# A gated graph network on Trainium2: all engines of the GRU stage in a written order, normalizing in halves, one staging place for two streams, weights turned in three places

## The chip, the core and the metric

The kernel runs on one core of a Trainium2 chip. The metric is device time in microseconds. The core's engines have names of their own in the profile: PE is TensorE (matmuls and transposes through the identity), ACT is ScalarE, DVE is VectorE, POOL is GpSimd, SP is SyncE, which here only issues DMAs.

## What is computed

The reference takes x [16, 1024, 128], an adjacency adj [16, 1024, 1024] of zeros and ones, a node mask (all ones) and weights. Two residual layers follow each other.

```python
# layer 0: pre-norm, four gated graph layers
h = relu(layernorm(x))
for i in range(4):
    m = adj^T @ (h @ weight[i])
    gx = m @ w_ih[i].T + b_ih[i];  gh = h @ w_hh[i].T + b_hh[i]
    r = sigmoid(xr + hr);  z = sigmoid(xz + hz);  n = tanh(xn + r * hn)
    h = (1 - z) * n + z * h
x = x + h * mask
# layer 1: pre-norm, four convolutions
h = relu(layernorm(x))
for i in range(4):
    h = batchnorm_over_batch_and_nodes(relu(adj @ (h @ W[i]) + b[i]))
out = x + h * mask
```

## The kernel before

There are two stages in one program. The GRU stage does layer 0, batch by batch, until about 1165 us; then the convolution stage does layer 1. The change lies in the GRU stage. A flag is computed beside it (`worst`, L1223): the largest low half of any word of adj, which says whether adj is exactly representable in the short type in which its rows are kept for layer 1. ACT reads such low halves with `glance` (L587), DVE with `look` (L611), one row block of 128 x 1024 at a time.

**Streams and clocks.** Two streams run against each other: A has the even batches, B the odd ones. One call of `half_step(one, two)` is a clock, counted from 3; at odd clocks `one` is A, at even clocks B. In a clock PE does the gates of `two` in two halves of 512 nodes (12 passes each, L982) and then the aggregation of `one` (32 matmuls of 128 x 512, L525): h, with nodes on the partitions, is split in a high and a low part, and each of the eight row blocks of adj meets both. h @ weight isn't computed: weight is folded into w_ih beforehand (`join_layer`, L487), so the gates take m through `w_mT`. A batch has four layers of one aggregation and one gate step each; a pair of batches takes eight clocks. I call the clock in which A does its fourth layer's gates 8k, for k = 1 to 7; there B aggregates its fourth layer. In 8k+1, B does its fourth gates and A aggregates the first layer of its next batch, and in 8k+2 B aggregates the first layer of its own.

**What a clock needs from the others.** ACT does for each half r = sigmoid (L994), tanh (L1000), z = sigmoid (L1001), and DVE the sums around them: two ahead of the tanh (L995, L996), then h − n (L1007, or L1005 in a batch's first layer), times z (L1008), plus n (L1009). Each gate has a single PSUM bank (`g_r`, `g_z`, `g_hn`, `g_xn`), so the second half's products wait until the first half's readers are done. The new h goes to node order through DRAM: DVE transposes blocks of 32 x 32 (L721), SP writes them out (L592) and reads them back (L599), ACT copies the high part (L915; L937 in a first layer, straight from y) and DVE subtracts to get the low part (L916, L941). At the end of an aggregation ACT copies m from PSUM in two halves (L954); the gates of the next clock need it.

**Work beside the gates.** A finished batch has its tail: sums with the mask (`tail_sums`), factors (a square root on ACT with its table load, L669), eight normalizing blocks (`norm_blocks`, ACT, L681), and stores. A coming batch has its x loaded, statistics, factors, and again eight blocks. An agenda, `at(clock, place, go)`, says in which clock and at which place of it each is issued; most are in the place "gap", between the halves of the aggregation. In 8k and 8k+1 the next batch's adjacency comes: `fetch` has SP load four row blocks of 512 KB into a staging tile of the stream (L573), POOL rounds them to the matmul's type (L578), ACT glances at them, and then the other four go into the same places. The low halves of A's last four are looked at by DVE, B's by ACT one clock later. The row blocks are also transposed on PE for layer 1, in the places where `feed.some` stands.

**What sets the order.** Up to clock 4 all engines run in the order written. From clock 5 on only PE, POOL and SP do (`tc.manual_schedule(engines=...)`, ahead of the loop); ACT and DVE are ordered by a scheduler, with `behind(...)` as a hint that something comes after a given instruction.

**Weights.** Three transposes give w_hhT (L470), three w_ihT (L474), one the graph weight (L479), each group with its own copy out; layer 1's are made halfway through clock 3's aggregation, layer 2's halfway through clock 4's, layer 3's after it.

Of the kernel before, what the change touches and what calls it, by code (L numbers as in the profile page):

```python
# [341 lines left out]
def exact_path(  # L342
# [123 lines left out]
    def turn_layer(prep, w_g, i):  # L466

        pt = tmp(f"pt_whh{i}")
        for g in range(3):
            nc.tensor.transpose(pt[:, g * P : (g + 1) * P], wns["hh", i][:, g, :], ident)  # L470
        nc.scalar.copy(w_hhT[:, i, :], pt[:, : 3 * P])
        pt = tmp(f"pt_wih{i}")
        for g in range(3):
            nc.tensor.transpose(pt[:, g * P : (g + 1) * P], wns["ih", i][:, g, :], ident)  # L474

        w_ihT = prep.tile([P, 3 * C], F32, tag="w_ihT", name=f"w_ihT{i}", bufs=1)
        nc.scalar.copy(w_ihT, pt[:, : 3 * P])
        pg = tmp(f"pt_g{i}")
        nc.tensor.transpose(pg[:, :P], w_g[:, i, :], ident)  # L479
        w_gT = prep.tile([P, P], F32, tag="w_gT", name=f"w_gT{i}", bufs=1)  # L480
        nc.scalar.copy(w_gT, pg[:, :P])
        turned[i] = w_gT, w_ihT
# [51 lines left out]
    with ExitStack() as st:  # L534
# [234 lines left out]
        written = [True]  # L769

        def behind(*inss):

            es = ExitStack()
            for ins in () if written[0] else inss:
                es.enter_context(tc.issue_after(ins.ins))
            return es

        class Stream:


            def __init__(self, first):
                self.b, self.i, self.tag = first, 0, "AB"[first % 2]
                self.opened, self.across, self.stage = None, False, None
                self.outs, self.split = [], []
# [31 lines left out]
            def load_ahead(self):  # L816
                self.next_x = load_x(self.b + 2, nc.gpsimd)

# [9 lines left out]
            def next_blocks(self):  # L828
                self.next_y = work.tile([P, N], F32, tag=f"y{self.tag}", name=f"y_in{self.b + 2}", bufs=1)
                norm_blocks(self.next_x, self.next_y, self.next_norm, range(NB))  # L830

            def plan(self, n, tail=None):

                if tail:
# [6 lines left out]
                    def blocks():  # L841
                        end["y"] = y_mid(b)
                        norm_blocks(xt, end["y"], end["norm"], range(NB))
# [4 lines left out]
                    at(n + 4, "gap", blocks)  # L848
                    at(n + 5, "mid", lambda: store_ymid(b, end["y"]))
                if self.b + 2 < B:  # L850
                    at(n + 5, "mid", self.next_load)
                    at(n + 5, "gap", self.next_sums)
                    at(n + 6, "gap", self.next_factors)
                    at(n + 7, "gap", self.next_blocks)

            def fetch(self):

                if self.i == 3 and self.b + 2 < B and not written[0]:
                    stage = turned_tile(f"stage{self.b + 2}").bitcast(F32)
                    self.stage = [stage[:, 2 * q : 2 * q + 2, :].rearrange("p a n -> p (a n)") for q in range(4)]  # L860
                    stage_rows(self.b + 2, self.stage, range(4))

            def first_four(self):
                if self.stage:
                    with behind(self.first_act):
                        glance(self.b + 2, self.stage, range(1))
                    self.rows = round_rows(self.b + 2, self.stage, range(4))

            def last_four(self):
                if self.stage:  # L870
                    with behind(self.first_act):
                        glance(self.b + 2, self.stage, range(1, 4))
                    stage_rows(self.b + 2, self.stage, range(4, NB))
                    self.rows += round_rows(self.b + 2, self.stage, range(4, NB))
                    b, stage, self.stage = self.b + 2, self.stage, None
                    if self is sb:

                        at(clock[0] + 1, "late", lambda: glance(b, stage, range(4, NB)))
                        return
                    with behind(self.last_dve):  # L880
                        for j in range(4, NB):
                            look(b, stage[j % 4], j)

            def take(self):
# [3 lines left out]
                return blocks_out(self.y, f"in{self.b}")  # L888

            def turned_away(self, i):  # L890

                return not written[0] and i < L

            def half_away(self, hf):

                if self.turned_away(self.i + 1 - hf):
# [11 lines left out]
            def split_back(self, g, *after):  # L908
                if self.outs:
                    cols = slice(g * HALF, (g + 1) * HALF)  # L910
                    hi, lo = (four_ways(t[:, cols]) for t in self.hw)
                    back = by_nodes(self.backs[g])
                    with behind(*after):
                        self.split = [
                            nc.scalar.copy(hi, back),  # L915
                            nc.vector.tensor_sub(lo, back, hi.bitcast(F32)),  # L916
                        ]
# [3 lines left out]
            def split_step(self):  # L921
                self.split = []
                if self.outs:
                    self.halves_back()
                    return
                nm = f"{self.b}_{self.i}"
                self.hw = hw_tiles(self.b, f"ghw{nm}")
                for g in range(NH):
                    if self.i > 0:
                        features_times(None, self.hT, self.hw, g, f"g{nm}")  # L930
                        continue
                    self.split_high(g)
                    self.split_low(g)
# [31 lines left out]
            def gate_step(self, hf, between=None, after=()):  # L965
# [26 lines left out]
                r = work.tile([P, HALF], F32, tag="r", name=f"r{nm}")  # L992
                z = work.tile([P, HALF], F32, tag="z", name=f"z{nm}")
                self.first_act = nc.scalar.activation(r, pr, AF.Sigmoid, bias=brz[:, 3 * i : 3 * i + 1])  # L994
                nc.vector.scalar_tensor_tensor(r, phn, b_hn(i), r, ALU.add, ALU.mult)  # L995
                self.mid_dve = nc.vector.tensor_add(r, pxn, r)  # L996
                if between:
                    between()
                with behind(*after[:1]):
                    nc.scalar.activation(r, r, AF.Tanh, bias=b_in(i))  # L1000
                self.last_act = nc.scalar.activation(z, pz, AF.Sigmoid, bias=brz[:, 3 * i + 1 : 3 * i + 2])  # L1001
                ho = self.new[:, cols]
                with behind(*after[1:]):
                    if across:
                        nc.vector.tensor_sub(four_ways(ho), hin, four_ways(r))  # L1005
                    else:
                        nc.vector.tensor_sub(ho, hin, r)  # L1007
                nc.vector.tensor_mul(ho, ho, z)  # L1008
                self.last_dve = nc.vector.tensor_add(ho, ho, r)  # L1009
# [4 lines left out]
            def finish(self):  # L1014
# [8 lines left out]
                ins = self.take()  # L1023
                h_in = self.hT
                outs = blocks_out(args[-1], f"out{args[0]}")
# [15 lines left out]

        def half_step(one, two, gated=None, halfway=None):

            feed.next_step()
            one.split = []
            if one.i == 0:
                two.fetch()
            due("ins")
            if one is sb and one.i == 0 or written[0] and one is sa:
                feed.jobs = transposes([(s.b, s.rows) for s in (sa, sb)])  # L1050
            if one.i > 0:
                one.split_step()
                two.fetch()
                feed.some(2)
            two.gate_step(0)
            two.half_away(0)
            two.first_four()
            if feed.full or (clock[0], "mid") in agenda:

                pace = small.tile([P, 1], F32, tag="pace", name=f"pace{clock[0]}")  # L1060
                nc.gpsimd.tensor_copy(pace, two.new[:, :1])
                feed.store()
                due("mid")
            due("outs")
            one.split_back(0, two.last_act, two.mid_dve)
            one.split_back(1, two.last_act, two.mid_dve)
            if one.i > 0:
                feed.some(1)
            two.gate_step(1, None, one.split)
            two.half_away(1)  # L1070
            with behind(two.first_act):
                due("late")
            if one.i == 0:
                feed.some(1)
            two.last_four()
            if gated:
                gated()
            if one.i == 0:
                with behind(two.last_m):
                    one.split_step()  # L1080
# [3 lines left out]
            with behind(two.last_act, two.last_dve, *one.split):  # L1084
                due("gap")
            feed.some(NB if written[0] and one is sa else 1)
# [6 lines left out]
        with tc.tile_pool(name="prep", bufs=1) as prep, tc.manual_schedule(engines=every):  # L1093
# [42 lines left out]
            turn_layer(prep, w_g, 0)  # L1136
# [58 lines left out]
            sb.agg_rows(range(4, NB))  # L1195

            def looks():
                for j in range(4, NB):
                    first_look(1, j, raw1[j])

            sa.plan(0)
            sb.plan(1)
            half_step(sa, sb, looks, lambda: turn_layer(prep, w_g, 1))
            join_layer(1)
            half_step(sb, sa, None, lambda: turn_layer(prep, w_g, 2))
            join_layer(2)
            turn_layer(prep, w_g, 3)
            join_layer(3)
        with tc.manual_schedule(engines={getattr(mybir.EngineType, e) for e in ("PE", "Pool", "SP")}):
            written[0] = False  # L1210
            for s in range(2, B // 2 * L):
# [302 lines left out]
```

## Time and profile before

| | us |
|---|---|
| median of three runs | 1789.59 (1788.88 to 1790.59) |
| the profiled execution | 1787.94 |
| its span | 1786.2 |
| PE busy in it | 1761.1 (99%) |
| DVE, ACT, POOL busy | 1254.0, 1107.5, 387.7 |
| time in which `g_r` waited for ACT's m | 30.6 in 61 waits of the weight load, the longest 1.8 |
| time in which ACT's glances waited for rows | 10.9 |

The granted TensorE clock is 0.998 in the profile. A line of the groups reads: source line, engine, operation, output <- inputs by the program's names, shapes, count, then busy time and mean duration in ns, then the idle time of the engine before them and what ended it. A line of the timeline reads: start and duration in us from the span's start, the engine, line and operation, the number of instructions in a row of that kind, and in brackets the idle time before with what ended it. Starts and durations of PE overlap, since its matmuls are pipelined; differences of starts are what counts there.

### The profile page before, as it was taken

The numbers are of one execution on the slowest core, as the hardware profiler recorded it, in microseconds if no ns is written. First come the engines' busy times: TensorE is split into PE (matmuls) and PEld (weight loads), VectorE is DVE, ScalarE is ACT, GpSimd is POOL, SyncE is SP. The second block draws the span as 40 slices with busy tenths as digits, with TensorE's granted clock in tenths as the row PEclk, the third lists the DMA queues.
The fourth block names the chain that finished last, engine by engine and source line by source line (L and its number), as shares of the span: only waits on it lengthen the run. The fifth ranks groups of instructions, "written<-read, shape, count | busy, mean of one in ns | idle before, by whom it ended". The sixth has DMA issues, their size and how long they took to land. (4 is left out here: it accounts for less than half of the span.)

```text
span 1786.2 us, 22134 instructions
## 1 busy us (share of the span) xinstructions
PE 1761.1 (99%) x6742; PEld 1193.5 (67%) x6742; DVE 1254.0 (70%) x2308; ACT 1107.5 (62%) x1717; POOL 387.7 (22%) x417
## 2 busy tenths in 40 slices
PE   9999999999999999999999999999999999999997
PEld 5556555565656565556565656577778888888886
DVE  7567867877776776877786776666666666666665
ACT  5346556556566555655655645476777767768765
POOL 4213323332322332422422333010100000000011
PEclk9999999999999999999999999999999999999999
DMA  7448677776776866776866867778766575767667
GB/s 254 113 123 294 168 205 245 205 210 224 224 200 216 229 198 203 244 204 185 286 173 172 266 185 215 274 266 313 276 220 246 206 248 208 248 224 239 244 216 270
DMA packets 362175, 399.09 MB, mean 223 GB/s; under 512 B 158028, under 2 KB 238704, under 8 KB 362048
## 3 DMA queue, kind: packets, MB, share of 16 engines
q1 hardware_dynamic: 341296, 322.54, 58.0%
q0 software_dynamic: 20224, 74.80, 11.4%
q8 instruction: 55, 0.90, 0.2%
q14 instruction: 72, 0.59, 0.1%
q10 hardware_dynamic: 528, 0.26, 0.0%
HBM read 266.95 MB, written 96.99 MB: 204 GB/s over the span
## 5 line engine op out<-in xcount | busy, mean ns | idle before, releaser
L525 PE MATMUL pm<-row,ghw 128*128 128x512 f32 x2048 | 506.8, 404 | 4.8 <-DVE ghw L916 4.1
L525 PEld LDWEIGHTS pm<-row,ghw 128*128 128x128 f32 x2048 | 384.6, 188 | 115.1 <-issue 29.4
L525 PE MATMUL pc_m<-wide,chw 128*128 128x512 f32 x1024 | 246.1, 395 | 0.0
L525 PEld LDWEIGHTS pc_m<-wide,chw 128*128 128x128 f32 x1024 | 190.4, 188 | 42.3 <-issue 4.3
L616 POOL CAST half<-row 128x1024 bf16<-128x1024 f32 x128 | 145.0, 1143 | 336.2 <-DMA adjT<-half 321.5
L525 PE MATMUL pc_g_r<-wide,chw 128*128 128x512 f32 x464 | 187.0, 403 | 0.3 <-ACT chw L502 0.3
L525 PE MATMUL pc_g_z<-wide,chw 128*128 128x512 f32 x464 | 181.0, 390 | 0.0
L995 DVE SCALAR_TENSOR_TENSOR r<-g_hn,vecs,r 128x512 f32<-128x512 f32 x128 | 95.1, 743 | 122.2 <-ACT r L994 76.5
L578 POOL CAST row<-stage 128x1024 fp32r<-128x1024 f32 x112 | 131.4, 1184 | 221.4 <-DMA stage<-in_adj_dram 171.3
L1001 ACT ACTIVATE z<-g_z,brz 128x512 f32<-128x512 f32 x128 | 87.4, 683 | 148.2 <-PE g_z L982 148.0
L954 ACT COPY m<-pm 128x512 f32<-128x512 f32 x128 | 68.5, 587 | 153.6 <-PE pm L525 153.5
L1000 ACT ACTIVATE r<-r,vecs 128x512 f32<-128x512 f32 x128 | 91.8, 717 | 114.4 <-DVE r L996 114.4
L1244 DVE CAST wide<-block 128x1024 fp32r<-128x1024 bf16 x160 | 109.8, 692 | 73.3 <-PE pc_m L525 49.4
L1244 DVE CAST wide<-packed 128x1024 fp32r<-128x1024 bf16 x160 | 110.2, 691 | 72.0 <-PE pc_g_z L525 54.0
L1007 DVE TENSOR_TENSOR h<-h,r 128x512 f32<-128x512 f32 x96 | 80.7, 841 | 100.2 <-ACT r L1000 100.2
L1242 ACT CAST wide<-packed 128x1024 fp32r<-128x1024 bf16 x96 | 100.6, 1048 | 58.9 <-PE pc_m L525 29.7
L982 PE MATMUL g_r<-m,w_mT 128*128 128x512 f32 x256 | 131.3, 594 | 3.5 <-ACT m L954 3.2
L1242 ACT CAST wide<-block 128x1024 fp32r<-128x1024 bf16 x96 | 100.6, 1049 | 52.6 <-PE pc_g_z L525 27.7
L982 PE MATMUL g_xn<-m,w_mT 128*128 128x512 f32 x256 | 130.8, 593 | 0.1
L982 PE MATMUL g_z<-m,w_mT 128*128 128x512 f32 x256 | 130.7, 592 | 0.0
L1292 DVE BATCH_NORM_STATS2 stats<-feat 128x6 f32<-128x512 f32 x128 | 84.1, 686 | 47.0 <-ACT feat L1291 45.9
L994 ACT ACTIVATE r<-g_r,brz 128x512 f32<-128x512 f32 x128 | 87.8, 686 | 37.4 <-PE g_r L982 37.1
(187 smaller groups left out, 2832.7 us busy)
## 6 DMA issues: line engine op xcount, KB each, us to landing
block<-adjT_d SPq DMA_DIRECT2D x256, 256.0 KB, 4.9
packed<-adjT_d SPq DMA_DIRECT2D x256, 256.0 KB, 5.6
stage<-in_adj_dram SPq DMA_DIRECT2D x120, 512.0 KB, 5.4
adjT_d<-adjT POOLq DMA_DIRECT2D x16, 2048.0 KB, 8.3
cross_h<-t_h SPq DMA_DIRECT2D x90, 256.0 KB, 3.2
n_h<-cross_h SPq DMA_DIRECT2D x360, 64.0 KB, 2.0
xmid_d<-x POOLq DMA_DIRECT2D x16, 512.0 KB, 6.0
y<-ymid_d POOLq DMA_DIRECT2D x16, 512.0 KB, 5.4
```

What stands on the lines that cost most here:

```text
L525: nc.tensor.matmul(pm[hf], hw[s][:, j * P : (j + 1) * P], rows[j][:, hf * HALF : (hf + 1) * HALF], start=(j == 0 and s == 0), stop=(j == N ...
L578: nc.gpsimd.tensor_copy(t, stage[j % 4])
L616: nc.gpsimd.tensor_copy(t, row.bitcast(F32))
L982: nc.tensor.matmul(po, wT[:, i, g * C : (g + 1) * C], rhs, start=start, stop=stop)
L994: self.first_act = nc.scalar.activation(r, pr, AF.Sigmoid, bias=brz[:, 3 * i : 3 * i + 1])
L995: nc.vector.scalar_tensor_tensor(r, phn, b_hn(i), r, ALU.add, ALU.mult)
L1000: nc.scalar.activation(r, r, AF.Tanh, bias=b_in(i))
L1001: self.last_act = nc.scalar.activation(z, pz, AF.Sigmoid, bias=brz[:, 3 * i + 1 : 3 * i + 2])
L1007: nc.vector.tensor_sub(ho, hin, r)
L1242: nc.scalar.copy(r, t)
L1244: nc.vector.tensor_copy(r, t)
L1292: nc.vector.bn_stats(stats[:, b * NH + hf, :], dst)
```

## The change

The order of the loop is written out for all engines up to clock 64; only the last gates are left to the scheduler as before. For that, `gate_step` is cut in pieces (`products`, `reset_gate`, `candidate`, `update_gate`, `less`, `mixed`), and the loop places them among the splits of the other stream (`high`, `low`), the glances, and the agenda's places.

- The eight normalizing blocks are issued four and four between r and tanh of both halves ("beside0", "beside1").
- The normalized x of the coming batch is transposed and written out (`ins_away`) at the end of clock n+7, not at the batch's change one clock later; the old batch's output goes out half by half in `half_away`.
- Both streams' rows are staged in one tile (`room[0]`). All four glances at the first rows follow z of the second half, and the second four rows are asked for after them. DVE's looks at A's last rows stand at the start of 8k+1; B's last glances in the gap of 8k+2.
- The places and counts of the row blocks' transposes on PE are others (`counts`); they begin at clock 8k+3.
- `turn_layer` becomes `turn_hh` and `turn_ih`; the latter puts w_ihT and the graph weight in one bank with one copy. hh is turned inside or halfway through an aggregation, ih ahead of one, the join comes halfway. Layer 3's turning moves to clock 5, and in clock 5 A's h takes the way through DRAM and not that over PE.
- `worst` follows the tail's sums instead of preceding a gate's chain, and in POOL's queue y's load for layer 1 comes before one store of transposed rows.

```diff
-    def turn_layer(prep, w_g, i):
+    def turn_hh(i):
         pt = tmp(f"pt_whh{i}")
...
+    def turn_ih(prep, w_g, i):
         pt = tmp(f"pt_wih{i}")
         for g in range(3):
             nc.tensor.transpose(pt[:, g * P : (g + 1) * P], wns["ih", i][:, g, :], ident)
-        w_ihT = prep.tile([P, 3 * C], F32, tag="w_ihT", name=f"w_ihT{i}", bufs=1)
-        nc.scalar.copy(w_ihT, pt[:, : 3 * P])
-        pg = tmp(f"pt_g{i}")
-        nc.tensor.transpose(pg[:, :P], w_g[:, i, :], ident)
-        w_gT = prep.tile([P, P], F32, tag="w_gT", name=f"w_gT{i}", bufs=1)
-        nc.scalar.copy(w_gT, pg[:, :P])
+        nc.tensor.transpose(pt[:, 3 * P :], w_g[:, i, :], ident)
+        both = prep.tile([P, 4 * C], F32, tag="w_both", name=f"w_both{i}", bufs=1)
+        nc.scalar.copy(both, pt)
...
-                    at(n + 4, "gap", blocks)
+                    at(n + 4, "beside0", lambda: blocks(0))
+                    at(n + 4, "beside1", lambda: blocks(1))
...
-                    at(n + 5, "gap", self.next_sums)
+                    at(n + 6, "start", self.next_sums)
                     at(n + 6, "gap", self.next_factors)
-                    at(n + 7, "gap", self.next_blocks)
+                    at(n + 7, "beside0", lambda: self.next_blocks(0))
+                    at(n + 7, "beside1", lambda: self.next_blocks(1))
+                    at(n + 7, "end", self.ins_away)
...
             def last_four(self):
                 if self.stage:
-                    with behind(self.first_act):
-                        glance(self.b + 2, self.stage, range(1, 4))
-                    stage_rows(self.b + 2, self.stage, range(4, NB))
-                    self.rows += round_rows(self.b + 2, self.stage, range(4, NB))
                     b, stage, self.stage = self.b + 2, self.stage, None
-                    if self is sb:
-                        at(clock[0] + 1, "late", lambda: glance(b, stage, range(4, NB)))
-                        return
-                    with behind(self.last_dve):
+                    glance(b, stage, range(4))
+                    stage_rows(b, stage, range(4, NB))
+                    self.rows += round_rows(b, stage, range(4, NB))
+
+                    def looks():
                         for j in range(4, NB):
                             look(b, stage[j % 4], j)
+
+                    if self is sa:
+                        at(clock[0] + 1, "start", looks)
+                    else:
+                        at(clock[0] + 1, "gap", lambda: glance(b, stage, range(4, NB)))
...
             def turned_away(self, i):
-                return not written[0] and i < L
+                return clock[0] > 3 and i < L
...
             due("ins")
+            due("start")
...
+            two.products(0)
+            two.reset_gate(0)
+            due("beside0")
+            two.candidate(0)
+            two.less(0)
+            one.high(0)
+            two.update_gate(0)
+            one.low(0)
+            two.mixed(0)
             two.half_away(0)
             two.first_four()
             if feed.full or (clock[0], "mid") in agenda:
+                mids(two)
+            one.high(1)
+            feed.some(counts[1])
+            two.products(1)
+            two.reset_gate(1)
+            due("beside1")
+            one.low(1)
+            two.candidate(1)
+            two.less(1)
+            two.update_gate(1)
+            two.last_four()
+            two.mixed(1)
+            two.half_away(1)
             due("outs")
+            due("gap")
+            due("end")
             if gated:
                 gated()
             one.agg_step(0)
             if halfway:
                 halfway()
-            feed.some(NB if written[0] and one is sa else 1)
+            feed.some(counts[2])
             one.agg_step(1)
             two.finish()
...
-            half_step(sa, sb, looks, lambda: turn_layer(prep, w_g, 1))
-            join_layer(1)
-            half_step(sb, sa, None, lambda: turn_layer(prep, w_g, 2))
-            join_layer(2)
-            turn_layer(prep, w_g, 3)
-            join_layer(3)
-        with tc.manual_schedule(engines={getattr(mybir.EngineType, e) for e in ("PE", "Pool", "SP")}):
+            first_step(sa, sb, looks, lambda: ahead(1))
+            first_step(sb, sa, lambda: turn_ih(prep, w_g, 2), lambda: ahead(2))
             written[0] = False
-            for s in range(2, B // 2 * L):
+            half_step(sa, sb, lambda: turn_ih(prep, w_g, 3), lambda: ahead(3))
+            half_step(sb, sa)
+            for s in range(3, B // 2 * L):
                 half_step(sa, sb)
                 half_step(sb, sa)
             assert not agenda, sorted(agenda)
+        with tc.manual_schedule(engines={getattr(mybir.EngineType, e) for e in ("PE", "Pool", "SP")}):
             sb.gate_step(0)
```

## The prediction

> **What bounds the kernel now.** I read in this order: busy shares, groups of TensorE (PE), waits, then PE's timeline around each wait. "Clock" means a half-step of the GRU loop, numbered as the code does (3 to 64); T0 is the first `g_r<-h` of a clock. The page and its groups:
>
> ```profile
> PE 1761.1 (99%) x6742; PEld 1193.5 (67%) x6742; DVE 1254.0 (70%) x2308; ACT 1107.5 (62%) x1717; POOL 387.7 (22%) x417
> L525 PE MATMUL pm<-row,ghw 128*128 128x512 f32 x2048 | 506.8, 404 | 4.8 <-DVE ghw L916 4.1
> ```
>
> PE is the engine, and its work is unchanged but for startup. So only its gaps count. A clock without a gap, and the next one:
>
> ```profile
> 279.04 1.02 PE L982 MATMUL g_r<-h,w_hhT 128*128 128x512 f32 x2
> ...
> 288.94 7.83 PE L525 MATMUL pm<-row,ghw 128*128 128x512 f32 x32
> 296.61 1.02 PE L982 MATMUL g_r<-h,w_hhT 128*128 128x512 f32 x2
> 298.61 1.12 PE L982 MATMUL g_r<-m,w_mT 128*128 128x512 f32 x2 [0.97 <-ACT m L954]
> ```
>
> From T0 to T0 it is 17.57 us (two halves of gates of 5.15, aggregation 7.27). Clock 17 waits for ScalarE's (ACT) copy of m; its T0s are 296.61 and 315.60, so it loses 1.42. Why the copy is late:
>
> ```profile
> 291.27 0.74 DVE L995 SCALAR_TENSOR_TENSOR r<-g_hn,vecs,r 128x512 f32<-128x512 f32 x1
> 293.24 0.72 ACT L1000 ACTIVATE r<-r,vecs 128x512 f32<-128x512 f32 x1 [1.97 <-DVE r L996]
> 293.87 1.04 ACT L587 ACTIVATE junk<-stage 128x1024 bf16<-128x1024 uint16 x1
> 294.91 3.17 ACT L681 ACTIVATE y_in<-x,ms_in,rs_in 128x128 f32<-128x128 f32 x8
> 297.99 1.04 ACT L954 COPY m<-pm 128x512 f32<-128x512 f32 x2
> ```
>
> ACT waited for VectorE (DVE), then did a glance and eight normalizing blocks, and m came after them. Every eighth clock has this queue. Another place is clock 59, where the flag's reduction stands on DVE ahead of the gates and waits for glances:
>
> ```profile
> 1040.23 0.30 DVE L1223 TENSOR_REDUCE worst<-low 128x1 f32<-128x144 f32 x1 [3.93 <-ACT junk L587]
> ...
> 1057.88 4.37 PE L525 MATMUL pm<-row,ghw 128*128 128x512 f32 x12 [2.08 <-DVE ghw L916]
> ```
>
> Over all: from clock 5's first aggregation matmul (94.91) to that of clock 64 (1146.99) lie 1052.08 us; 59 clocks of 17.573 are 1036.8. **15.3 us are stalls.** By clock: 59 has 4.3; 17 1.42, 33 1.23, 41 1.84, 57 1.43 (m or h_in late); 11, 19, 27, 35, 43, 49, 51 .4 to 1.0 (mostly the low half of hw, L916, late on DVE); 64 .6. Most clocks have none. The second stage (1165 on) is not touched.
>
> **What the Trainium skill says.** "Perfetto Trace Analysis", § Optimization Strategy, has one find the gaps on the most contended engine; the trace agrees that PE's 99% hides 15 us of them. "SBUF — State Buffer", § Who interferes with whom: a DVE instruction with two SBUF inputs and a GpSimd instruction that reads SBUF exclude each other. The trace agrees: L1008 takes .69 alone, 1.52 while GpSimd (POOL) casts rows at L578. "ScalarE: Activation LUTs", § What ACT_TABLE_LOAD costs, gives about 1283 ns; this trace has 1283. The number of loads stays.
>
> **Part 1, weights turned in three places.** Before, PE between its streams:
>
> ```profile
> 80.22 0.81 PE L487 MATMUL pt_wm<-w_ihT,w_gT 128*128 128x384 f32 x2
> 80.86 0.49 PE L470 MATMUL pt_whh<-ident,wn_hh 128*128 128x128 f32 x3
> 81.70 0.55 PE L474 MATMUL pt_wih<-ident,wn_ih 128*128 128x128 f32 x3 [0.35 <-ACT w_mT L488]
> 82.08 0.33 PE L479 MATMUL pt_g<-ident,w_g 128*128 128x128 f32 x1
> 83.04 0.91 PE L487 MATMUL pt_wm<-w_ihT,w_gT 128*128 128x384 f32 x2 [0.62 <-ACT w_gT L481]
> 83.79 1.39 PE L498 MATMUL hw_g<-ident,h 128*128 128x128 f32 x8
> 85.01 1.02 PE L982 MATMUL g_r<-h,w_hhT 128*128 128x512 f32 x2
> ```
>
> From clock 4's aggregation (real start 71.68) to clock 5's T0 at 85.01 are 13.33. After: aggregation 7.26, join .64, three hh transposes .33: 8.23. Layer 3's turning moves to clock 5, and its eight feature transposes go (1.2), since A's new hw then travels through DRAM; its halves are due only ten us later. So −5.1. Clock 3's aggregation (from 50.85) sheds seven transposes (.76) and two gaps of .4 from start to start (waits of .24), and gains three and four transposes (.33, .44): −.8. Clock 4 gains four ahead of its aggregation (+.44), clock 5 four and the join (.44 + .64 = +1.1). Layer 1's hh transposes at 37 add .33, mostly inside a wait of .47 at 44.8. Sum −.8 + .4 − 5.1 + 1.1 = **−4.4**, all on PE and so on the path. If the copies don't return in time for the transposes, one gap of .3 to .6 each comes back: bounds −5.0 to −3.0.
>
> **Part 2, written order, blocks in halves.** The eight blocks of 3.17 now lie four and four between r and tanh, where DVE's sums take longer anyhow; four cost ACT 1.6 and tanh waits for DVE until about then. ACT's queue in clock 8k (m copies, table load 1.28, r, four blocks, tanh, hi, z, hi, r, four blocks, tanh, z, four glances of 1.17) then, by the durations shown and T0=0: r0 ends 2.9, DVE's two sums 4.6, tanh0 to 5.3, second half's sums (DVE: less .69, lo, mul, add, transpose, two sums, one of them stretched by .8) to 11.0, tanh1, z1 to 12.3, glances to 17.0. m is wanted by 17.57+.24. No stall, slack .8. The late lows of clocks 8k+3 have written places ahead of the mul: stalls gone. L1223 moves to the tail's sums after the transpose: at most 1 us of DVE wait, PE unaffected. y's load in clock 60 moves past a store on POOL's queue: the .6 goes; if that were wrong, .6. All gains of this part: **−15.3**, if nothing new comes.
>
> **Part 3, one stage, glances after z.** This adds waits, which the trace of before doesn't show. The second four rows may only be fetched into a place when its glance is done; glances end at 13.5, 14.6, 15.8, 17.0, instead of beginning at 287.20 − 279.04 = 8.2. SP's queue holds nothing long ahead of them. SP's issues of rows and what it takes for one to land, from the line's own view:
>
> ```profile
> DMA to landing us min/median/max: 3.5/5.3/8.6
> ```
>
> Row 7, the last, took 4.0 to 5.8 before. So row 7 lands at 21.1 to 22.9, and its look (DVE, 1.2) ends at 22.3 to 24.0. In clock 8k+1 the looks stand on DVE ahead of the gates' first sum; behind them is the whole gate chain of stream B, so call their end s. From s: two sums 1.55 and tanh .7 (s+2.3), seven DVE instructions at pitches of .61 to .70 (4.6), tanh .65, z .6, four glances 4.7, .3 for hand-overs: ACT is free for m at s+13.1. T0 of 8k+2 is 35.14 and m may start at +.24 without loss. With s=22.4: 35.5−35.4=.1. **The unknown is contention**: B's rows land 24.5 to 29 and POOL casts them (L578) just while DVE does less, lo, mul, add of the first half; each that meets a cast is .8 longer (1.52 against .69). Two or three do: 1.6 to 2.4. Bounds: .1 (none meets, rows early) and 3.4 (s at 23.5, three met, and z0's bank, wanted by PE at 26.15, late by .6); not below zero: a gap can't be negative, and those of before are counted in part 2. I take 1.9 per eight clocks; seven pairs of batches (clocks 8 to 56): **+13.3**.
>
> What else moves costs nothing: next x dumped a clock earlier (two DVE transposes of .65 in a clock with several us of DVE idle; if that cover were gone, 1.3 per pair), t_out within clock 8k (same count); adjacency transposes start a clock later on PE (same number, in places that have their rows; a row missing would cost its landing, at most 1 us per pair).
>
> **Sum.** −4.4 −15.3 +13.3 = −6.4. The profiled execution took 1787.94 (span 1786.2): 1781.5. The median of the runs is 1789.59, 1.65 above it, so the forecast as a median is 1783.2.
>
> **Rivals.**
> Forecast (.45): new waits of about 1.9, range 1.0 to 2.5 per pair: 1777 to 1788.
> *Written order leaves nearly no stall* (.25): casts and sums miss each other, rows land early, .3 per pair: 2 instead of 13.3; −17.6: 1772. For it: rows' latencies at 3.5 are in the trace, and POOL is 22% busy. Against: before, L1008 averages .84, so a fifth of its instructions do meet a cast.
> *The one stage turns the chain late, slower* (.18): row 7 can't be asked for before the last glance, its look blocks DVE ahead of B's gates, B's glances wait for z, and m for these. At 3.9 per pair, 27.3 − 19.7 = +7.6: 1797. It decides from 19.7/7 = 2.8 per pair on (break-even), by .2% from 3.3. For it: every link is a written order with no slack beyond .2. Against: 3.9 needs the slowest landings and four meetings in each pair.
> *The waits just eat the gains* (.12): 2.8 per pair, 1789.6. That the change does nothing is thereby included.
> I count .2% (3.6 us) as what a measurement of this kernel can tell from no change. Below 1786.0 lie the second case and three quarters of the first: .59; between, the rest of the first and the last: .23; above 1793.2 the slower one: .18. Range 1771 to 1796: it leaves out the best of the second case and half of the slower one.
>
> **What would show it.** Right: clock 5's T0 about 5.5 earlier; no idle of PE at 8k+1 or 8k+3 and none after L1223; a wait of `g_r<-m` for ACT's m at T0 of clocks 10, 18, 26 and so on of 1 to 2.5. Wrong: that wait under .5 (second rival) or over 2.8 (third), DVE's first sum of 8k+1 beginning well before or after 22.4, L1223's reduction ahead of a gate again, or new gaps of PE in clocks without rows. The prediction is most wrong if the looks start late for a reason other than the row: then all seven pairs shift together.

## The result and the profile after

The changed kernel takes **1791.24 us** (median of 22 runs, 1788.37 to 1798.02) against 1788.39 for the kernel before (22 runs, 1785.18 to 1790.81): ratio **1.0020**, 95% interval 1.0014 to 1.0026. It is slower by 2.85 us; the forecast was 6.4 faster. The profiled execution took 1789.26 (span 1787.5), so the trace below shows 1.3 us of the difference. The changed kernel's runs spread more, and this execution lies 2.0 below their median. One run of the experiments, of the flag's reduction, fell in a slow state (3028.68 us at a granted clock of 0.556) and is left out of its median.

The page of the changed kernel, to be held against the first two lines shown of before (L525 is now L524, L916 L926):

```profile
PE 1759.3 (98%) x6734; PEld 1191.7 (67%) x6734; DVE 1305.9 (73%) x2310; ACT 1107.6 (62%) x1713; POOL 379.3 (21%) x417
L524 PE MATMUL pm<-row,ghw 128*128 128x512 f32 x2048 | 503.6, 402 | 0.7 <-DVE ghw L926 0.6
```

The late low halves (4.1 us of idle before) are down to 0.6. What PE waits for instead, from the waits of the whole span (total, times, longest):

```profile
PE g_z L993 <- ACT z L1020: 5.0, 8, 0.7
PE g_hn L993 <- DVE r L1012: 4.6, 6, 1.2
PE g_r L993 <- ACT m L955: 2.9, 4, 1.0
```

The first two are waits inside the gates; before, the first came to 0.8 and the second did not occur. PE's timeline of clock 17, the counterpart of the clock shown of before:

```profile
293.36 1.02 PE L993 MATMUL g_r<-h,w_hhT 128*128 128x512 f32 x2
...
301.54 1.13 PE L993 MATMUL g_hn<-h,w_hhT 128*128 128x512 f32 x2 [1.15 <-DVE r L1012]
...
304.18 1.12 PE L993 MATMUL g_z<-h,w_hhT 128*128 128x512 f32 x2 [0.66 <-ACT z L1020]
```

The m at the clock's start is in time now. But the second half's `g_hn` and `g_z` wait for the first half's banks. DVE's timeline of the same place two periods later (clock 33, T0 at 580.12) says why:

```profile
580.90 1.22 DVE L610 TENSOR_REDUCE low<-stage 128x1 f32<-128x1024 uint16 x1 [1.60 <-DMA stage<-in_adj_dram]
582.40 1.22 DVE L610 TENSOR_REDUCE low<-stage 128x1 f32<-128x1024 uint16 x1 [0.28 <-DMA stage<-in_adj_dram]
584.84 2.47 DVE L610 TENSOR_REDUCE low<-stage 128x1 f32<-128x1024 uint16 x2 [1.22 <-DMA stage<-in_adj_dram]
587.23 0.74 DVE L1012 SCALAR_TENSOR_TENSOR r<-g_hn,vecs,r 128x512 f32<-128x512 f32 x1
```

DVE, otherwise idle, waits for row after row of A, and the first sum of B's gates, which frees `g_hn`, stands behind the last of them.

A ledger of PE's lost time: for each clock the time from its T0 to the next, less the 17.573 of a clock without a gap, summed by the clock's place in its period (us; k = 1 to 7):

| | T0 of clock 6 | 8k+1 | 8k+2 | 8k+3 | 8k+4, 8k+5 | clocks 6 to 63 | T0 of clock 64 |
|---|---|---|---|---|---|---|---|
| before | 102.61 | 6.59 | 0.10 | 7.94 | 0 | 14.64 | 1136.48 |
| changed | 98.23 | 12.60 | 2.45 | 3.83 | 0.89 | 19.78 | 1137.25 |

The opening gives 4.37, the loop loses 5.14 more than before: +0.77 at clock 64. Here clock 3 is the first of the loop, and a loss is booked on the clock that holds it.

### The profile page after: what moved, and what is told of

It reads as the page before. It is cut to its first block, busy times and chain, and to the rows that moved or that the text cites. A ratio compares the mean times of both kernels' runs of the same rounds, so it can differ in the third digit from the quotient of the medians.

```text
span 1787.5 us, 22335 instructions
## 1 busy us (share of the span) xinstructions
PE 1759.3 (98%) x6734; PEld 1191.7 (67%) x6734; DVE 1305.9 (73%) x2310; ACT 1107.6 (62%) x1713; POOL 379.3 (21%) x417
## 5 line engine op out<-in xcount | busy, mean ns | idle before, releaser
L524 PE MATMUL pm<-row,ghw 128*128 128x512 f32 x2048 | 503.6, 402 | 0.7 <-DVE ghw L926 0.6
L524 PEld LDWEIGHTS pm<-row,ghw 128*128 128x128 f32 x2048 | 383.8, 188 | 106.6 <-issue 29.2
L524 PE MATMUL pc_m<-wide,chw 128*128 128x512 f32 x1024 | 245.3, 395 | 0.0
L524 PEld LDWEIGHTS pc_m<-wide,chw 128*128 128x128 f32 x1024 | 190.4, 188 | 41.9 <-issue 3.8
L524 PE MATMUL pc_g_r<-wide,chw 128*128 128x512 f32 x464 | 186.9, 403 | 0.3 <-ACT chw L501 0.3
L524 PE MATMUL pc_g_z<-wide,chw 128*128 128x512 f32 x464 | 181.0, 390 | 0.0
L1033 DVE TENSOR_TENSOR h<-h,z 128x512 f32<-128x512 f32 x128 | 107.8, 842 | 6.8 <-ACT z L1020 0.2
```

The lines of the kernel that those rows point to most:

```text
L524: nc.tensor.matmul(pm[hf], hw[s][:, j * P : (j + 1) * P], rows[j][:, hf * HALF : (hf + 1) * HALF], start=(j == 0 and s == 0), stop=(j == N ...
L1033: nc.vector.tensor_mul(ho, ho, self.z)
```

## The experiments

Theory after the result: A's last row lands late, DVE's looks at it stand ahead of the sum that frees a bank, and PE waits for the bank. Rivals: the chain up to m is the bound wherever the looks stand; or the stretching of DVE by POOL's casts, as forecast; or the two parts of the change work against each other. Ratios are to the kernel before, with 95% intervals.

**The weights' part alone**, put on the kernel before:

```diff
-            half_step(sa, sb, looks, lambda: turn_layer(prep, w_g, 1))
-            join_layer(1)
-            half_step(sb, sa, None, lambda: turn_layer(prep, w_g, 2))
...
+            half_step(sa, sb, looks, lambda: ahead(1))
+            half_step(sb, sa, lambda: turn_ih(prep, w_g, 2), lambda: ahead(2))
...
+            half_step(sa, sb, lambda: turn_ih(prep, w_g, 3), lambda: ahead(3))
```

> The kernel before with the weights' part of the change alone (turning in three places, A's h through DRAM in clock 5). If the trace of the changed kernel is read rightly, this is worth 4.4 us by itself: clock 6 begins 4.4 us earlier and everything after as in the kernel before, ratio to before 0.9975. If the gain depends on the written order of ACT and DVE, or is given back at the next batch's rows, clock 6 is earlier but clock 17 isn't, ratio 1.000.

Measured: 1780.88 us, ratio 0.9959 (0.9945 to 0.9973). Clock 6 begins at 98.51, 4.1 earlier, and clock 64 at 1131.17, 5.3 earlier. The gain is real, doesn't need the written order, and isn't given back. It is more than the 4.4 expected: 6.6 in the runs. The trace has 1.2 of it inside the loop; why is not shown.

**The order alone**: the changed kernel with the weights as before.

```diff
-            first_step(sa, sb, looks, lambda: ahead(1))
-            first_step(sb, sa, lambda: turn_ih(prep, w_g, 2), lambda: ahead(2))
+            first_step(sa, sb, looks, lambda: turn_layer(prep, w_g, 1))
+            join_layer(1)
+            first_step(sb, sa, lambda: None, lambda: turn_layer(prep, w_g, 2))
...
```

> The changed kernel with the weights' part undone: turned as in the kernel before, so that the written order, the halves, the early dump and the one stage stand alone. If the two parts add up, clock 6 begins as in the kernel before, the waits of the loop are those of the changed kernel (19 to 22 us of PE) and it is 4.4 us (up to 6) slower than the changed kernel: 0.4 to 0.5% slower than before, ratio 1.004 to 1.006. Rival: the two parts are coupled (an earlier start meets worse landings); then it is near the kernel before, 1.000 to 1.002.

Measured: 1796.61, ratio 1.0042 (1.0028 to 1.0055). In its trace clocks 8k+1 lose 18.8 and the whole loop 24.5, more than expected. One item of the weights' part stayed in it, A's h through DRAM in clock 5: clock 6 begins at 101.23, 1.4 earlier than before, where the expectation had it at the same time. The product of the two ratios, which counts that item twice, is 1.0001; with the intervals of the parts that does not differ from 1.0020. So there is a gain of 0.4% and a loss of 0.4% or more, not two small effects. A coupling isn't needed for that, but one of a few us isn't excluded (the loop loses 24.5 here, 19.78 in the changed kernel).

**The looks behind the first sums, first try.**

```diff
-                        at(clock[0] + 1, "start", looks)
+                        at(clock[0] + 1, "start", lambda: looks(range(4, 6)))
+                        at(clock[0] + 1, "beside0", lambda: looks(range(6, NB)))
```

> The changed kernel with the looks at A's rows 6 and 7 behind DVE's two first sums of clock 8k+1 instead of ahead of them. Theory: the sums that free the banks of g_hn and g_z stand behind a row that lands late. Then the 12.6 us of PE waits in the clocks 9, 17, ... 57 fall below 2, the waits for m in the next clocks stay at about 0.3 each, and the kernel is 10 to 12 us faster than the changed one: ratio to before 0.995. Rival: the chain sum, tanh, less, ... second tanh, z, glances is the bound, wherever the looks stand, and the wait moves to m at the start of clocks 10, 18, ...: these rise from 0.35 to 1.5 to 2 each, and the time stays within 2 us of the changed kernel: ratio to before 1.000 to 1.002.

Measured: 1838.99, ratio 1.0286 (1.0272 to 1.0300). Neither theory said so. "beside0" is issued after B's rows are asked for into the same places, so these two looks read B's rows 2 and 3 and not A's 6 and 7. DVE's timeline of clock 9 shows what they waited for:

```profile
165.79 2.46 DVE L610 TENSOR_REDUCE low<-stage 128x1 f32<-128x1024 uint16 x2 [9.28 <-DMA stage<-in_adj_dram]
168.16 0.68 DVE L1030 TENSOR_TENSOR h<-h,r 128x512 f32<-128x512 f32 x1
```

It decides nothing between the theories, but it is the same mechanism enlarged: a look that waits 9.28 us in DVE's queue cost 8 to 10 us in each of seven clocks.

**The same, with B's rows 2 and 3 asked for after the looks.**

```diff
-                    stage_rows(self.b + 2, self.stage, range(4))
+                    stage_rows(self.b + 2, self.stage, range(4 if self is sa else 2))
...
             due("beside0")
+            if two is sb and two.stage:
+                stage_rows(two.b + 2, two.stage, range(2, 4))
```

> The looks at A's rows 6 and 7 behind DVE's two first sums of clock 8k+1 again, this time with B's rows 2 and 3 asked for after them, so that the looks read A's rows. Theory (sums behind a late row free the banks late): the PE waits within the gates of clocks 8k+1 (12.6 in all) fall below 2, those for m at the start of 8k+2 stay at 0.3 to 0.6: 8 to 11 us below the changed kernel, ratio to before 0.995 to 0.997. Rival (the chain to m is the bound wherever the looks stand): m's waits rise to 1.5 to 2 each, and the time is within 2 us of the changed kernel.

Measured: **1776.93**, ratio 0.9940 (0.9923 to 0.9956), 14.3 below the changed kernel, where 8 to 11 were expected; the two traces show 11.8 of it. DVE in clock 33 (T0 at 574.70):

```profile
577.39 1.22 DVE L610 TENSOR_REDUCE low<-stage 128x1 f32<-128x1024 uint16 x1 [0.40 <-DMA stage<-in_adj_dram]
578.52 0.74 DVE L1013 SCALAR_TENSOR_TENSOR r<-g_hn,vecs,r 128x512 f32<-128x512 f32 x1
579.37 0.69 DVE L1014 TENSOR_TENSOR r<-g_xn,r 128x512 f32<-128x512 f32 x1
579.98 1.21 DVE L610 TENSOR_REDUCE low<-stage 128x1 f32<-128x1024 uint16 x1
582.05 1.22 DVE L610 TENSOR_REDUCE low<-stage 128x1 f32<-128x1024 uint16 x1 [0.87 <-DMA stage<-in_adj_dram]
```

The row is as late as ever, and DVE still waits 0.87 for it, but behind the sums. Clocks 8k+1 lose 0.0 instead of 12.6, and 8k+2 loses 2.17, much as before this edit (2.45). The rival (m is the bound wherever the looks stand) is out. This run doesn't separate the bank from m as what would stop PE, since both follow from DVE's first sum.

**The rows asked for earlier**, with the looks where the change put them.

```diff
             due("beside1")
+            if two is sa and two.stage:
+                glance(two.b + 2, two.stage, range(2))
...
-                    glance(b, stage, range(4))
-                    stage_rows(b, stage, range(4, NB))
+                    if self is sa:
+                        stage_rows(b, stage, range(4, 6))
+                        glance(b, stage, range(2, 4))
+                        stage_rows(b, stage, range(6, NB))
...
```

> The changed kernel with ACT's glances at A's first two rows ahead of the second tanh of clock 8k, where ACT idles for 2.5 us, and the rows 4 and 5 asked for ahead of the other two glances. Theory: the landing of row 7 follows its issue; it is asked for 2.3 us earlier (15.5 instead of 17.8 after clock 8k's T0), lands 1 to 2.3 earlier, the looks end as much earlier, and the PE waits of clocks 8k+1 fall from 12.6 to 2 to 5 in all: 8 to 10 us below the changed kernel, ratio to before 0.996. Rival: the DMA queues' own pace sets the landing: row 7 lands within 0.5 us of where it does now, gain below 3 us.

Measured: **1774.08**, ratio 0.9920 (0.9905 to 0.9935), 17.2 below the changed kernel and more than expected. The two traces show 11.7 of it: the changed kernel's was 2.0 faster than its median, this one 3.5 slower. Clocks 8k+1 lose 0.48. From the traces, row 7 (us after clock 8k's T0, seven periods): before it was asked for at 14.5 to 16.0 and landed at 20.0 to 20.8; changed, 16.3 to 17.8 and 22.2 to 23.8; here, 15.0 to 15.6 and 20.7 to 21.6. The landing follows the asking; the rival (the queues' pace alone sets it) is out.

**B's last glances out of m's way.**

```diff
-                        at(clock[0] + 1, "gap", lambda: glance(b, stage, range(4, NB)))
+                        at(clock[0] + 1, "beside1", lambda: glance(b, stage, range(4, NB)))
```

> The changed kernel with B's last four glances between r and tanh of the second half of clock 8k+2, where ACT idles for 5 us, instead of after z in its gap. Theory: m is late at the start of clocks 11, 19, 27, ... because four glances stand ahead of it. Then the 3.8 us of waits there vanish, nothing comes in their place: ratio to before about 0.9995, 3 to 4 us below the changed kernel. Rival: DVE's chain, lengthened by POOL's casts, is the bound of that clock; then the tanh comes no earlier, m is wanted at the same time anyway and at least 1 us of each wait stays: 0 to 1 us below the changed kernel.

Measured: 1791.98, ratio 1.0024 (1.0017 to 1.0030): no gain. Clocks 8k+3 lose 0 instead of 3.83, as the theory had it, but 8k+2 loses 5.17 instead of 2.45, 8k+4 and 8k+5 lose 3.5 instead of 0.9, and 8k+1 loses 13.9 instead of 12.6. In this trace the waits moved; what brought each of the new ones is not shown.

**The same edit on the kernel with early rows**, and on it also z ahead of the copy of the high half:

```diff
             two.less(0)
-            one.high(0)
             two.update_gate(0)
+            one.high(0)
```

> A's early glances (1774.1 alone) with B's last glances between r and tanh of 8k+2, without the swap of z and the high copy. The three together gave 1783.4. If the swap was what cost (the high and low parts come too late for the aggregation), this gives 1769 to 1772; if the place of B's last glances costs (they hold up the tanh of 8k+2 behind them), it stays at 1778 to 1784.

> A's first two glances ahead of the second tanh in clock 8k (which alone gave 1774), B's last four glances between r and tanh in 8k+2, and z of the first half ahead of the copy that waits for the DRAM round trip. If the waits are separate, those of 8k+3 (4.45 in that trace) and 8k+4, 8k+5 (2.4) go, and the time is 1766 to 1769, ratio 0.988 to 0.990. If one hides behind the other and they only move, it stays at 1772 to 1776.

Measured: 1776.87 without the swap (0.9932, 0.9916 to 0.9949) and 1783.41 with it (0.9975, 0.9961 to 0.9989); the early rows alone had 1774.08. PE's waits in the loop, first without, then with the swap:

```profile
PE g_z L998 <- ACT z L1025: 3.9, 6, 1.6
PE pm L524 <- DVE ghw L931: 0.8, 1, 0.8
```

```profile
PE g_r L998 <- ACT m L960: 3.0, 7, 0.6
PE pm L524 <- DVE ghw L931: 3.0, 5, 1.5
```

The wait for z behind the high copy, which waits for the DRAM round trip, is gone; the low halves are late in its place. The expectation of 1766 to 1772 was wrong for both, and neither lies in the range of its rival. In the runs the swap costs 6.5 us, in the traces 0.7, since the trace without it is of the slowest of its four runs (1781.57). Why removing one of these small waits gains nothing is not shown.

**The flag's reduction alone**, on the kernel with the weights' part:

```diff
-    nc.vector.tensor_reduce(worst, low, axis=AX.X, op=ALU.max)
...
+            at(60, "gap", lambda: nc.vector.tensor_reduce(worst, low, axis=AX.X, op=ALU.max))
```

> The kernel before with the weights' part and with the reduction of the flag (L1223) in the gap of clock 60 instead of ahead of the gate's sums in clock 58; ACT and DVE else in the scheduler's order. If that one instruction is what stops PE at clock 59, its 4.3 to 4.8 us go in full: 4 to 5 us below the kernel with the weights' part alone (1780.9), 1776, ratio to before 0.9935. If the clock is late for its glances anyway, 0 to 1 us.

Measured: 1776.86 (median of the three runs left, 1774.73 to 1779.00), ratio 0.9944 (0.9924 to 0.9963). Clock 59 loses 0.13 (4.77 without the edit). The gain over the weights' part alone is 4.0 us, as expected; the intervals of the ratios overlap, but all three runs lie below that kernel's five (1780.17 to 1782.85).

**B's last glances a clock later still**, on both cures; and the same with B's first glances two and two:

```diff
-                        at(clock[0] + 1, "gap", lambda: glance(b, stage, range(4, NB)))
+                        at(clock[0] + 2, "gap", lambda: glance(b, stage, range(4, NB)))
```

> The changed kernel with the early glances at A's first rows (1774.1 alone), the looks at A's rows 6 and 7 behind the two first sums (1776.9 alone), and B's last glances a clock later, in the gap of 8k+3, where nothing waits for them; z stays behind the copy of the high part. If what is left are the waits for m behind glances, those of 8k+3 (3.5 to 4.5) go and the others stay small: 1768 to 1771, ratio 0.989 to 0.991. If the gap of 8k+3 with its square root and table load is full, m is late at 8k+4 instead and it stays at 1773 to 1777.

> The same, and the last two of B's first four glances, with the rows asked for after them, between r and tanh of clock 8k+2 instead of ahead of m at its start. The waits for m at the start of 8k+2 (about 2 in all) go, rows 6 and 7 of B land some 4 us later with slack ahead of their use: 1766 to 1769. If the rows come too late for B's aggregation in 8k+2, a wait of PE for them of 1 us or more per pair appears there, and it is slower than the kernel without this step.

Measured: 1848.25 (1.0329, 1.0311 to 1.0346) and 1849.70 (1.0339, 1.0322 to 1.0357). Both expectations failed. Clock 12 of the first loses 12.1. SP's timeline there, then ACT's, then PE's wait for z in the loop:

```profile
188.02 3.73 SPq L598 DMA_DIRECT2D n_h<-cross_h  x8
205.41 2.59 SPq L616 DMA_TRANSPOSE adjT<-half  x2
208.11 0.52 SPq L591 DMA_DIRECT2D cross_h<-t_h  x1
```

```profile
203.88 1.06 ACT L586 ACTIVATE junk<-stage 128x1024 bf16<-128x1024 uint16 x1
204.85 0.18 ACT L586 ACTIVATION_READ_ACCUMULATOR junk<-stage 128x1 f32 x1
220.78 0.62 ACT L925 CAST ghw<-n_h 128x512 fp32r<-128x512 f32 x1 [10.45 <-DMA n_h<-cross_h]
```

```profile
PE g_z L999 <- ACT z L1026: 57.3, 7, 8.7
```

The staging place is the buffer that the transposed rows need next. SP's queue stood 13 us, from the end of its loads at 191.75 to the moment the last glance was done, and the round trip of h stood behind in the same queue; the copy of the high half waited for it, z stood behind the copy, and PE waited for z's bank. Whether B's first glances are better two and two can't be told beside that.

**Both cures together**, B's last glances where the change has them (the diffs of the early rows and of the looks, nothing else):

> The changed kernel with both cures of the late row: A's early glances (1774.1 alone) and the looks at A's rows 6 and 7 behind the two first sums (1776.9 alone), B's last glances left in the gap of 8k+2. Each alone took the 12.6 us of the clocks 8k+1 away, so the two together can't take it twice: what the second adds is the contention that is left at the start of 8k+2 and 8k+3 (2.1 and 4.5), of which at most half goes. 1772 to 1775, ratio 0.991 to 0.993. If the two hinder each other (DVE's less and lows fall behind the looks), 1776 to 1780.

Measured: **1772.73**, ratio 0.9914 (0.9901 to 0.9928): 18.5 below the changed kernel, 0.9% below the kernel before, and within the range expected. It is the lowest median of the study, but the runs don't tell it from the early rows alone (0.9905 to 0.9935). Clocks 6 to 63 lose 5.45. Two small edits of the kernel before, the weights and the flag's reduction, had come to 1776.86 without the written order.

## Why the prediction was wrong

**What held.** The opening: −4.4 forecast, −4.37 at clock 6, and −4.1 where it stood alone; clock 5 begins 5.51 earlier (5.5 forecast). The stall of L1223 is gone, and so are the late lows of 8k+3. (Of the small losses of before that I listed, clock 43 has none; the 15.3 hold.) The length of the chain from s (DVE's first sum in 8k+1) to the end of the glances was put at 13.1; it is 13.04 to 13.12 in all seven periods.

**The step that failed in the mechanism: the value taken for s, "With s=22.4".** My range for the end of the last look was 22.3 to 24.0, and I took its early end. Measured, s is 23.37 to 25.0, 24.41 in the mean, and in six of the seven periods it is past the late end. Row 7 took 5.7 to 6.6 us to land, 6.0 in the mean, where 22.4 had 4.0 in it. The 4.0 came from rows asked for 3.7 us behind the one ahead. Four asked for 1.2 us apart land 1.2 to 2.9 apart, 2.0 in the mean, so that the fourth takes 2.3 us longer in the mean than the first (3.5 to 4.1). Glances that ended at 16.2 to 17.7 fit the 17.0 forecast.

**Where it is paid.** I had named z's bank, "wanted by PE at 26.15, late by .6", as a far bound, and booked the loss at m. Measured, most of it is paid earlier, at the banks. In the trace the loss of clock 8k+1 is s − 22.62 to within 0.03: s = 23.37, 24.12, 24.70, 24.98 lost 0.75, 1.50, 2.08, 2.37. That is 12.6 us instead of nothing. My chain to m was nevertheless sized rightly: 8k+1 and 8k+2 together lose s + 13.1 − 35.4 to within 0.07 in all seven periods, 15.05 us. By that sum m would have cost about as much if no bank had stopped PE. So the late s is the cause, and the bank is only where most of it is paid.

**Contention, "1.6 to 2.4", wasn't there.** From s to the second tanh no sum was stretched in any of the seven periods, since B's first row landed only when the first half's sums were nearly over (592.5 in clock 33, where the last of them began at 591.56), and the second half's two sums, which read PSUM, weren't longer beside the casts (0.71 and 0.69); less and mul of the second half were (1.52 and 1.34 in clock 33), but they lie behind the tanh. The Trainium skill's section on who interferes with whom ("SBUF — State Buffer"), by which a DVE instruction with two inputs in SBUF contends with a GpSimd instruction that reads SBUF and one with a single such input does not, fits both; I had the wrong instructions under it. In clocks 8k+2 it is there (mul 1.52, add 1.41 in clock 34).

**The step that failed in the sum: clock 8k+3, taken as free of stalls.** I had counted the late lows there as gone and put the glances that now stand ahead of m at nothing. It loses 3.83 because m stands behind B's last glances; with these moved it loses 0. In clock 35 (T0 at 617.69, m wanted 0.24 later) ACT has:

```profile
617.84 1.06 ACT L586 ACTIVATE junk<-stage 128x1024 bf16<-128x1024 uint16 x1
618.90 1.05 ACT L955 COPY m<-pm 128x512 f32<-128x512 f32 x2
```

And clock 64 still loses its 0.6 at m. I had it for a late load of y, but the cast ahead of m waits for the aggregation (ACT's timeline):

```profile
1137.04 1.05 ACT L1370 CAST chw<-y 128x1024 fp32r<-128x1024 f32 x1 [6.04 <-PE pm L524]
1137.99 1.07 ACT L955 COPY m<-pm 128x512 f32<-128x512 f32 x2
```

**The sum.** New waits per pair: 1.9 forecast, (12.60 + 2.45 + 3.83 + 0.89)/7 = 2.8 measured, or 19.8 us in place of 13.3. Clocks 8k+1 and 8k+2 have 15.05 of them, only 1.75 above the forecast, and that nearness is luck: an s that came 2.0 us late stands against a contention of 1.6 to 2.4 that didn't come. Clocks 8k+3 and 8k+4 have the other 4.7, where I had nothing. The 2.8 are the case I gave .12 ("the waits just eat the gains"), reached by the mechanism of the slower rival: the looks ahead of B's gates. One of my signs misled: the losses at the start of 8k+2, 0.31 to 0.38, are under the .5 that was to speak for the rival with nearly no stall, since most had been paid a clock earlier. The profiled difference of +1.3 is −4.37 + 5.14, and 0.5 more behind clock 64. The other 1.5 us of the medians are not in the one trace; that rows land later in other executions would fit the wider spread, and wasn't shown.

## What to carry to other kernels

An instruction that waits for a DMA belongs behind the work that others wait for, not ahead of it in the same queue: moving two looks behind two sums, with the two loads that had to follow them, was worth 14 us. When transfers are asked for one behind another's release, price the last by the pace of the row of them and not by the latency of one with a pause ahead, and take the late end if the queue behind it has no slack. A large change that moves nothing is worth taking apart: here a gain of 0.4% and a loss of as much lay in one diff, and with two small edits of the order the whole came to 0.9% below the kernel before.

## What the runs showed of the hardware that I had not expected

- Four loads of 512 KB, asked for 1.2 us apart, took 3.5 to 4.1 us for the first and 5.7 to 6.6 for the fourth.
- Four glances at a staging place, moved one clock (17.6 us) later, stopped SP's queue for 13 us at the next use of the place and cost 10.4 to 12.4 us in each of seven periods.
